# Two residual graph-attention layers on one core: the third of seven products is split into seven small ones too, and tiles and PSUM banks are shared out anew

## The chip, the core and the metric

The kernel runs on one NeuronCore of a Trainium2 chip. The metric is the device time of one execution in microseconds (us), the median of several runs. Five engines work side by side, each through its own queue in order: TensorE (PE) multiplies matrices and writes into PSUM, VectorE (DVE) and ScalarE (ACT) read PSUM and work elementwise, GpSimd (POOL) works elementwise on SBUF, and SyncE (SP) issues the DMA transfers here. They wait for each other by semaphores. [...]

## The reference

There are 128 graphs of 128 nodes with 512 features, one adjacency matrix `adj` for all of them, and two layers in fp32. Cut to what matters:

```
# layer 0
q, k, v = x @ Wq0.T, x @ Wk0.T, x @ Wv0.T
rel = adj.T * (q @ k.T);  rel = rel / norm(rel, axis=2)
x1  = layernorm(x + rel @ v)
# layer 1: 8 heads of 64
q, k, v = x1 @ Wq1 + bq1, x1 @ Wk1 + bk1, x1 @ Wv1 + bv1
w   = softmax(q_h @ k_h.T / 8 + where(adj == 0, -1e9, 0))
out = layernorm(x1 + concat_h(w @ v_h))
```

## The kernel before

**Groups and projections.** The kernel takes four graphs at a time: 32 groups `g` of 512 tokens. Wq0 and Wk0 are multiplied into one matrix at the start, so a group needs five products of a 512 x 512 weight with its 512 x 512 tokens: `m` and `v0` in layer 0, `q`, `k` and `v1` in layer 1. Each is an instance of `Projection`, 160 in all.

**Seven products.** A projection is not done as eight products of halves but as seven, P1 to P7 (Winograd's form of Strassen's scheme), on sums of weights (`wc`, seven tiles made once, `weight_sums`) and on sums of tokens (`tx` and `tx1`, four tiles made for each group by `token_sums`). `product` issues one of them as four matmuls of 256 columns (L327). P1, P6, P7 and P4 go into bank `a` in turn and partly add up there, P5 and P3 into bank `b`. `empty` copies a bank to SBUF on ACT (L335, L338); `add` adds a bank to an SBUF tile on DVE (L342).

**P2 is made from seven products of quarters.** The second product is split once more in the same way: `inner_product` issues one matmul of 128 columns (L360), `inner` does seven of these in four steps of 3, 2, 1 and 1 and adds each to the projection's output on DVE (L374 to L390). They use sums of weight quarters (`wd`, `inner_weight_sums`) and of token quarters (`ux`, L234 to L237, on POOL). All seven share three slots of one bank `pc`. In group 0 `m` and `v0` are plain: their P2 is four ordinary matmuls.

**Order.** Nothing is left to a scheduler: the emission order is a list of steps. A round `r` has 35 steps, seven for each projection. `dense` holds the projections' products at fixed places in those seven (P1 at 0, P5 at 1, P6 at 3, P3 at 5, P7 at 6, P4 at 9, that is at 2 of the next one), with the inner steps at the places of `INNER`. `short` holds everything else at places that hand-set tables give: `ZERO` for layer 0, `STEADY`, `QUICK` and `LAST` for the softmax and output of layer 1 in ordinary rounds, the last but one group, and the last. Round `r` makes `m` and `v0` of group r+1, and `q`, `k`, `v1` of group r; the softmax of a group runs on into the next two rounds. Each engine takes its own instructions in this order.

**Softmax and rows.** For each graph `b` of a group: `attn_scores` (PE into banks `ps`, then DVE), `attn_max` (DVE), `attn_exp` (ACT), `attn_spill` and `attn_stage` (DMA to HBM and back, for a layout), `attn_transpose` (DVE into `wT`), `attn_out` (PE into `po`, then DVE), `attn_back` and `attn_rows` (DMA to HBM and back: rows `o` of softmax times v, and rows `xr` of x1), `attn_sum` (DVE multiplies `o` by the softmax's divisors, POOL adds the bias and `o` to `xr`), `attn_stats`, `attn_norm`, `attn_write`. Layer 0 has `l0_score` (banks `pst`), `l0_norm` (bank `pn`, from squares `sq` made on POOL), `l0_out`, `l0_rstd`, `l0_layernorm`; `x1_spill` and `x1_stage` bring x1 to HBM and back for `x1_transpose`, `x_transpose` does the same for the next x.

**Buffers.** Eight PSUM banks: two of `ps_a` (bank `a`), one of `ps_b` (bank `b`), five of `ps_m` (all else). SBUF tiles are named by tags; a tile with a tag used before waits for the end of all use of the tile before it. `o` and `xr` have two tiles each of their own, and `self.s`, half of which holds P5 and half P6, has a tile with the tag `s`.

Of the kernel before, what the change touches and what calls it, by code (L numbers as in the profile page):

```python
# [18 lines left out]
def kernel(  # L19
# [32 lines left out]
    ps_b = ctx.enter_context(tc.tile_pool(name="ps_b", bufs=1, space=bass.MemoryType.PSUM))  # L52
    ps_m = ctx.enter_context(tc.tile_pool(name="ps_m", bufs=5, space=bass.MemoryType.PSUM))
# [87 lines left out]
    wd = {n: const.tile([P, 3, P], F32, name=f"wd_{n}") for n in wc}  # L141

    def inner_weight(key, i):
        if i >= 5:
            return wd[key][:, i - 5]
        e, d = {1: (0, 0), 2: (0, 1), 3: (1, 0), 4: (1, 1)}[i]
        return wc[key][:, 1, d, e * P:(e + 1) * P]

    def inner_weight_sums(key, eng):
        w = [None] + [inner_weight(key, i) for i in range(1, 8)]  # L150
        eng.tensor_tensor(w[5], w[3], w[4], op=ALU.add)
        eng.tensor_tensor(w[6], w[5], w[1], op=ALU.subtract)
        eng.tensor_tensor(w[7], w[1], w[3], op=ALU.subtract)
        eng.tensor_tensor(w[3], w[2], w[6], op=ALU.subtract)
# [63 lines left out]
    def token_sums(t, xT, dh):  # L218

        if dh == 0:  # L220
            nc.vector.tensor_tensor(t[:, 0], quarter(xT, 0, 1), quarter(xT, 0, 0), op=ALU.subtract)
        else:
            nc.vector.tensor_tensor(t[:, 1], quarter(xT, 1, 1), t[:, 0], op=ALU.subtract)
            nc.gpsimd.tensor_tensor(t[:, 2], quarter(xT, 1, 1), quarter(xT, 0, 1), op=ALU.subtract)
            nc.gpsimd.tensor_tensor(t[:, 3], quarter(xT, 1, 0), t[:, 1], op=ALU.subtract)

    def inner_token(xT, i):
        d, t = {1: (0, 0), 2: (1, 0), 3: (1, 1), 5: (0, 1)}[i]
        return xT[:, 2 + d, t, :]

    def inner_token_sums(u, xT):

        eng = nc.gpsimd
        eng.tensor_tensor(u[:, 0], inner_token(xT, 5), inner_token(xT, 1), op=ALU.subtract)  # L234
        eng.tensor_tensor(u[:, 1], inner_token(xT, 3), u[:, 0], op=ALU.subtract)
        eng.tensor_tensor(u[:, 2], inner_token(xT, 3), inner_token(xT, 5), op=ALU.subtract)
        eng.tensor_tensor(u[:, 3], inner_token(xT, 2), u[:, 1], op=ALU.subtract)  # L237

    def x_inner(g):
        UX[g] = one.tile([P, 4, P], F32, tag="ux", name=f"ux_{g}")  # L240
        inner_token_sums(UX[g], XT[g])

    def x1_inner(g):
        UX1[g] = one.tile([P, 4, P], F32, tag="ux1" if g < NG - 1 else "ux", name=f"ux1_{g}")
        inner_token_sums(UX1[g], X1T[g])

    def x_transpose(g, dh, h):
        if dh == 0 and h == 0:

            XT[g] = one.tile([P, C, G, P], F32, tag="xT" if g else "x1T", name=f"xT_{g}")  # L250
            TX[g] = one.tile([P, 4, 2, HF], F32, tag="tx" if g else "tx1", name=f"tx_{g}")
        transpose_quarter(XT[g], g, h, dh)
        if h:
            token_sums(TX[g], XT[g], dh)
# [11 lines left out]
    def x1_transpose(g, dh, h):  # L266
        if dh == 0 and h == 0:

            X1T[g] = one.tile([P, C, G, P], F32, tag="x1T" if g < NG - 1 else "xT", name=f"x1T_{g}")
            TX1[g] = one.tile([P, 4, 2, HF], F32, tag="tx1" if g < NG - 1 else "tx", name=f"tx1_{g}")  # L270
        transpose_quarter(X1T[g], g, h, dh)
        if h:
            token_sums(TX1[g], X1T[g], dh)

    def graph(g, b):
        return X[g, b // 2][:, b % 2, :]

    class Projection:
# [8 lines left out]
        def begin(self):  # L287
# [5 lines left out]
            if k == "v1":  # L293

                self.s0 = one.tile([P, 2, HF], F32, tag="rel", name=f"s0_{self.name}")
# [3 lines left out]
            self.s = one.tile([P, 2, 2, HF], F32, tag="s", name=f"s_{self.name}")  # L299
# [41 lines left out]
        def add(self, eh, th, bank, s):  # L341
            nc.vector.tensor_tensor(self.out(eh, th), bank, self.s[:, s], op=ALU.add)  # L342

        def quarters(self, j):

            y = self.y.rearrange("p a b -> p (a b)" if self.wide else "p c b n -> p (c b n)")
            y = y.rearrange("p (j n) -> p j n", n=P)
            s0 = y if self.kind != "v1" else self.s0.rearrange("p m (t n) -> p (m t) n", n=P)
            w = C if self.kind != "v1" else 2
            e, t = j  # L350
            if not self.wide:
                e, t = t, e
            i, k = e + t * C, e + t * w
            return (y[:, i], s0[:, k]) if j != (1, 1) else (y[:, 0:i + 1:i], s0[:, 0:k + 1:k])

        def inner_product(self, i, slot, start=False):
            l, r = inner_weight(self.kind, i), self.u[:, {5: 0, 6: 1, 7: 2, 4: 3}[i]] if i >= 4 else inner_token(self.xT, i)
            if self.wide:
                l, r = r, l
            nc.tensor.matmul(self.c[:, slot, :], l, r, start=start, stop=True, skip_group_check=True)  # L360

        def inner(self, n):

            add = nc.vector.tensor_tensor
            self.u = (UX if self.kind in ("m", "v0") else UX1)[self.g]
            if n == 0:
                if self.kind == "v1":
                    self.place()
                self.c = ps_m.tile([P, 3, P], F32, tag="m", name=f"pc_{self.name}")
                self.inner_product(1, 0, True)  # L370
                self.inner_product(5, 1)
                self.inner_product(2, 2)
                y, s0 = self.quarters((1, 1))
                add(y, self.c[:, 0:2], s0, op=ALU.add)  # L374
                y, _ = self.quarters((0, 0))
                add(y, self.c[:, 2], y, op=ALU.add)
            elif n == 1:
                self.inner_product(6, 0)
                self.inner_product(3, 1)
                y, s0 = self.quarters((0, 1))  # L380
                add(y, self.c[:, 0], s0, op=ALU.add)
                add(y, self.c[:, 1], y, op=ALU.add)
            elif n == 2:
                self.inner_product(7, 0)
                y = self.last_quarter()
                add(y, self.c[:, 0], y, op=ALU.add)
            else:
                self.inner_product(4, 0)
                y, s0 = self.quarters((1, 0))
                add(y, self.c[:, 0], s0, op=ALU.add)  # L390

        def last_quarter(self):
            return self.quarters((1, 1))[0][:, 1]

        def step(self, i):
            if i == 1:
                self.begin()
                self.a = ps_a.tile([P, 2, HF], F32, tag="a", name=f"pa_{self.name}")
                self.product(1, self.a, True)
                self.empty(self.s0, self.a, 0)  # L400
            elif i == 5:
                self.b = ps_b.tile([P, 2, HF], F32, tag="b", name=f"pb_{self.name}")
                self.product(5, self.b, True)
                self.empty(self.s[:, 0], self.b, 1)
            elif i >= 10:
                if not self.plain:
                    self.inner(i - 10)
            elif i == 2:
                if self.plain:
                    d = ps_m.tile([P, 2, HF], F32, tag="m", name=f"pd_{self.name}")  # L410
                    self.product(2, d, True)
                    nc.vector.tensor_tensor(self.s0, d, self.s0, op=ALU.add)
            elif i == 6:
                self.product(6, self.a, False)
                self.empty(self.s[:, 1], self.a, 0)
            elif i == 3:
                self.product(3, self.b, False)
                self.add(0, 1, self.b, 1)
            elif i == 7:
                self.product(7, self.a, False)  # L420
                self.add(1, 1, self.a, 0)
# [150 lines left out]
    def attn_rows(g, b):  # L572
        o = two.tile([P, A, H // 2, Q], F32, tag="o", name=f"o_{g}_{b}")
        nc.sync.dma_start(o.rearrange("p f a r -> p (f a r)"), OD.pop((g, b)).rearrange("p f d -> p (f d)"))
        xr = two.tile([P, D], F32, tag="xr", name=f"xr_{g}_{b}")
        nc.sync.dma_start(xr, X1D[g, b // 2][b % 2])
        SOFT[g, b] = o, xr, SOFT[g, b][1]

    def attn_sum(g, b):

        o, xr, rs = SOFT[g, b]
        f = o.rearrange("p f a r -> p (f a) r")
# [4 lines left out]
        nc.gpsimd.tensor_tensor(xr_, xr_, o, op=ALU.add)  # L587
# [92 lines left out]
    def last_store(g, b):  # L680
# [13 lines left out]
        ((10.5, 10.5, 10.5, 11), 13.5, (22.5, 21.5, 20, 19.5), 24, (28.5, 27), (31, 30.5), (35, 32.5), (38, 40.5, 42.5, 44.5)),  # L694
# [3 lines left out]
        (32, (35.5, 35.5, 36, 36, 36), (36, 36), 41.5, (43.5, 49, 49, 52, 56.5, 59.5, 61, 62.5)),  # L698
        (32, (32.5, 40, 40, 42, 42), (40, 42.5), 44.5, (47, 49, 50, 53, 59, 65, 66, 68.5)),
        (49, (50.5, 50.5, 50.5, 52, 52), (52, 54.5), 54.5, (59, 67, 67.5, 69.5, 75, 78, 78, 80)),  # L700
        (49, (53, 53, 54, 56, 57), (59, 59), 61, (65, 67, 68.5, 71.5, 76.5, 82, 82, 83.5)),
    )
    QUICK = (
        (31.5, (32, 33.5, 33.5, 34, 36), (33.5, 36), 40.5, (42, 43.5, 44, 47.5, 48.5, 50.5, 52, 52.5)),
        (35.5, (36, 37, 37, 37, 37), (39.5, 39.5), 41, (45.5, 47.5, 47.5, 50, 52.5, 53.5, 55.5, 62.5)),
        (36, (38, 41, 41, 41, 41), (41, 41), 45.5, (47.5, 52, 57.5, 57.5, 57.5, 59, 61.5, 64)),
        (37.5, (39, 40, 44, 49, 49), (46, 49), 51.5, (53, 54.5, 60, 63, 63, 67.5, 68.5, 68.5)),
# [128 lines left out]
```

## Time and profile before

| | us |
|---|---|
| runs | 2457.88, 2459.82, 2459.85 |
| median | 2459.82 |
| profiled execution, its own time | 2458.22 |
| its span in the trace | 2456.3 |
| granted TensorE clock, mean | 0.998 |

The page of the profiled execution gives each engine's busy time, share of the span and count of instructions. A group's row names a line of the kernel, the engine, the operation, output and inputs with their shapes, how often it ran, its busy time, the mean duration of one in ns, the idle time just before it, and what ended that. A row of waits is: who waited for whom, total us, times, longest. Matmul records overlap, so what one costs is read from the distance of starts. An fp32 matmul shows as two records, each with a weight load (PEld).

### The profile page before, as it was taken

To read this page: it belongs to the slowest core of one execution; us is meant where nothing else is said; L and a number is where in the kernel's file an instruction comes from. 1 tells how busy PE (TensorE), PEld (TensorE's weight loads), DVE (VectorE), ACT (ScalarE), POOL (GpSimd) and SP (SyncE) were. 2 spreads that over 40 slices of the span, in tenths; PEclk is the share of its full clock that TensorE was granted. 3 is DMA by queue.
4 is the path that set the end of the run, shared out by engine and by line. 5 is a ranking of instruction groups with operands and counts; after the bars stand their busy time and mean duration, and the time that the engine had idled before them with its cause. 6 is when DMAs were issued, how large, how long until landed. Compare 5 with 4: busy or idle time off the path is not lost.

```text
span 2456.3 us, 44484 instructions
## 1 busy us (share of the span) xinstructions
PE 2435.0 (99%) x15604; PEld 2123.7 (86%) x15604; DVE 1738.2 (71%) x3505; ACT 1000.4 (41%) x3211; POOL 952.3 (39%) x1478
## 2 busy tenths in 40 slices
PE   8999999999999999999999999999999999999997
PEld 6888888888888888888888888888888888888886
DVE  5566777767777767777677777677776777776777
ACT  1234343433443343434434443434344343434354
POOL 4423433434434334334344343443333433434434
PEclk9999999999999999999999999999999999999999
DMA  7446656666565666556665656655566556566564
GB/s 160 104 129 183 164 161 169 164 183 171 162 165 157 173 187 164 163 162 165 187 165 165 171 153 174 189 163 163 159 164 189 158 166 172 158 176 182 150 172 133
DMA packets 508577, 404.93 MB, mean 165 GB/s; under 512 B 37568, under 2 KB 424768, under 8 KB 508352
## 3 DMA queue, kind: packets, MB, share of 16 engines
q1 hardware_dynamic: 508352, 402.08, 60.2%
q8 instruction: 122, 2.00, 0.4%
q14 instruction: 103, 0.84, 0.1%
HBM read 237.31 MB, written 164.63 MB: 164 GB/s over the span
## 4 chain that ended last, share of the span: by engine, by line
PE 98%; DVE 1%; POOL 0%; issue 0%; DMA 0%; POOLq 0%; ACT 0%; SPq 0%; DVEq 0%
PE pa_v L327 18%; PE pa_q L327 9%; PE pa_k L327 9%; PE pa_m L327 9%; PE pb_v L327 9%; PE ps L499 5%; PE po L557 5%; PE pst L434 5%; PE pb_q L327 5%; PE pb_k L327 4%; PE pb_m L327 4%; PE po L479 4%; PE pc_v L360 4%; PE pc_q L360 2%; PE pc_k L360 2%; PE pc_m L360 2%
## 5 line engine op out<-in xcount | busy, mean ns | idle before, releaser
L585 POOL TENSOR_TENSOR xr<-xr,bv_b 128x512 f32<-128x512 f32 x124 | 158.4, 1278 | 626.0 <-DMA xr<-x1d 204.8
L525 ACT ACTIVATE w<-w,nmax 128x128 f32<-128x128 f32 x992 | 384.2, 392 | 11.7 <-DVE nmax L518 11.7
L587 POOL TENSOR_TENSOR xr<-xr,o 128x512 f32<-128x512 f32 x124 | 157.5, 1270 | 532.7 <-issue 457.5
L327 PE MATMUL pa_v<-wc_v,tx 128*128 128x256 f32 x1536 | 363.7, 380 | 0.0
L327 PEld LDWEIGHTS pa_v<-wc_v,tx 128*128 128x128 f32 x1536 | 282.1, 190 | 33.7
L474 ACT ACTIVATE xr<-xr,sh,rstd 128x512 f32<-128x512 f32 x124 | 100.9, 814 | 377.6 <-POOL sh L469 377.4
L525 ACT ACTIVATION_READ_ACCUMULATOR w<-w,nmax 128x1 f32 x992 | 189.1, 191 | 0.0
L327 PE MATMUL pa_m<-tx,wc_m 128*128 128x256 f32 x768 | 181.7, 379 | 0.8 <-DVE yT L342 0.8
L327 PE MATMUL pa_k<-tx,wc_k 128*128 128x256 f32 x768 | 181.7, 379 | 0.0
L327 PE MATMUL pa_q<-tx,wc_q 128*128 128x256 f32 x768 | 181.6, 379 | 0.0
L327 PEld LDWEIGHTS pa_q<-tx,wc_q 128*128 128x128 f32 x768 | 143.3, 190 | 43.8 <-issue 28.9
L508 DVE SCALAR_TENSOR_TENSOR w<-ps,mask 128x512 f32<-128x512 f32 x248 | 154.2, 684 | 15.6 <-PE ps L499 15.6
L338 ACT ACTIVATE qT<-pa_q,bq_sb 128x256 f32<-128x256 f32 x128 | 53.6, 470 | 271.9 <-PE pa_q L327 271.9
L544 DVE STREAM_TRANSPOSE wT<-wl 128x1024 f32<-128x1024 f32 x124 | 154.0, 1242 | 5.7 <-DMA wl<-wd 4.6
L518 DVE TENSOR_REDUCE nmax<-w 128x4 f32<-128x512 f32 x248 | 157.2, 676 | 0.0
L327 PEld LDWEIGHTS pa_m<-tx,wc_m 128*128 128x128 f32 x768 | 141.1, 190 | 17.8 <-DVE yT L342 1.2
L327 PEld LDWEIGHTS pa_k<-tx,wc_k 128*128 128x128 f32 x768 | 141.0, 190 | 16.6 <-issue 0.2
L560 DVE STREAM_TRANSPOSE oT<-po 128x512 f32<-128x512 f32 x124 | 88.8, 716 | 79.5 <-PE po L557 76.0
L335 ACT COPY yT<-pa_m 128x512 f32<-128x512 f32 x64 | 37.7, 590 | 231.2 <-PE pa_m L327 231.2
L499 PE MATMUL ps<-kT,qT 64*128 64x128 f32 x1984 | 129.5, 279 | 0.0
L499 PEld LDWEIGHTS ps<-kT,qT 64*128 64x128 f32 x1984 | 117.4, 187 | 11.2 <-issue 10.8
L479 PE MATMUL po<-v,rel 128*128 128x512 f32 x256 | 125.4, 592 | 0.0
(229 smaller groups left out, 5432.9 us busy)
## 6 DMA issues: line engine op xcount, KB each, us to landing
wd<-w SPq DMA_DIRECT2D x248, 256.0 KB, 3.1
wl<-wd SPq DMA_DIRECT2D x496, 128.0 KB, 3.1
xl_x<-in_x_dram SPq DMA_DIRECT2D x256, 128.0 KB, 6.7
x<-in_x_dram SPq DMA_DIRECT2D x64, 512.0 KB, 4.9
x1d<-x SPq DMA_DIRECT2D x64, 512.0 KB, 2.8
xl_h<-x1d SPq DMA_DIRECT2D x256, 128.0 KB, 3.5
od<-oT SPq DMA_DIRECT2D x496, 64.0 KB, 1.8
o<-od SPq DMA_DIRECT2D x124, 256.0 KB, 3.2
```

What stands on the lines that cost most here:

```text
L327: nc.tensor.matmul(bank[:, m, :], l[:, k, m * P:(m + 1) * P], r[:, k, :], start=start and m == 0 and k == 0, stop=(m == 1 and k == 1), ski ...
L360: nc.tensor.matmul(self.c[:, slot, :], l, r, start=start, stop=True, skip_group_check=True)
L434: nc.tensor.matmul(p, XT[g][:, dc, b, :], YT[g][:, dc, b, :], start=(dc == 0), stop=(dc == C - 1))
L479: nc.tensor.matmul(p, REL[g][0][:, b, :], V0[g][:, b, :], start=True, stop=True)
L499: nc.tensor.matmul(p[s][:, :, a, :], QT[g][r, a, b, :], KT[g][r, a, b, :], start=True, stop=True)
L508: nc.vector.scalar_tensor_tensor(w[:, s].rearrange("p q a r -> p (q a r)"), p[s].rearrange("p q a r -> p (q a r)"), HD ** -0.5, mask, op0= ...
L518: nc.vector.tensor_reduce(nmax[:, s * (H // 2):(s + 1) * (H // 2)], w[:, s].rearrange("p q a r -> p a q r"), axis=AX.XY, op=ALU.max, negat ...
L525: nc.scalar.activation(w[:, s, :, a, :], w[:, s, :, a, :], AF.Exp, bias=nmax[:, i:i + 1], accum_out=sums[:, i:i + 1])
L544: nc.vector.transpose(wT, SOFT[g, b][0].rearrange("p a i r -> p i a r"))
L557: nc.tensor.matmul(p[s * HD:(s + 1) * HD, a, :], V1[g][:, b, h * HD:(h + 1) * HD], wT[:, s * (H // 2) + a].rearrange("p q t -> p (q t)"), ...
L585: nc.gpsimd.tensor_tensor(xr, xr, bv_b, op=ALU.add)
L587: nc.gpsimd.tensor_tensor(xr_, xr_, o, op=ALU.add)
```

## The change

P3 is split as P2 is. `inner_weight`, `inner_weight_sums`, `inner_token`, `inner_token_sums` and `inner` get a number `o` (2 or 3) for the outer product. `wd` and `ux` double, and there are two banks `pc2` and `pc3` in place of `pc`. The plain projections make P3 with four ordinary matmuls in a bank of its own.

Since P3 no longer adds up in bank `b`, the sums are formed elsewhere: P5 is copied twice (`s01`, `s11`), P6 is added to `s01` on DVE and no longer copied by ACT, P7 is added to `s11`. For `v1` (but for the last group) these two lie in a shared tile (`shared`), for the others in the projection's own output, so that the tag `s` goes. The shared tile has the tag `yT` and also holds the rows `xr` of graphs 0 and 1; `room` places the other rows `o` and `xr` in tiles with the tags `tx` and `x`, and at the end in the weights of `m` and `v0`. The tags `o` and `xr` go.

`attn_rows` is cut in two: `attn_res`, which loads `xr`, comes at step `RES` = 59 for graphs 0 and 1. The first token sum is made on POOL from the third group of x on, and for x1; the inner weight sums of `v0` and `m` are made on DVE, those of the others later. `ps_b` goes and `ps_m` has six banks. Places in `ZERO`, `STEADY`, `QUICK` and `LAST` are changed, a few by several steps; the order of P1, P5, P6, P7 and P4 is not.

```
-    ps_b = ctx.enter_context(tc.tile_pool(name="ps_b", bufs=1, space=bass.MemoryType.PSUM))
-    ps_m = ctx.enter_context(tc.tile_pool(name="ps_m", bufs=5, space=bass.MemoryType.PSUM))
+    ps_m = ctx.enter_context(tc.tile_pool(name="ps_m", bufs=6, space=bass.MemoryType.PSUM))
...
     def inner_weight_sums(key, eng):
+        for o in (2, 3):
+            w = [None] + [inner_weight(key, o, i) for i in range(1, 8)]
+            eng.tensor_tensor(w[5], w[3], w[4], op=ALU.add)
...
+    def token_sums(t, xT, dh, eng=nc.gpsimd):
         if dh == 0:
-            nc.vector.tensor_tensor(t[:, 0], quarter(xT, 0, 1), quarter(xT, 0, 0), op=ALU.subtract)
+            eng.tensor_tensor(t[:, 0], quarter(xT, 0, 1), quarter(xT, 0, 0), op=ALU.subtract)
...
         transpose_quarter(XT[g], g, h, dh)
+        if dh == 1 and g:
+            inner_token_sums(UX[g], XT[g], 2 + h)
         if h:
-            token_sums(TX[g], XT[g], dh)
+            token_sums(TX[g], XT[g], dh, nc.gpsimd if g > 1 else nc.vector)
...
+    def shared(r):
+        if r not in SX:
+            t = one.tile([P, 2, 2, D], F32, tag="yT", name=f"sx_{r}")
+            SX[r] = t[:, 0], t[:, 1].rearrange("p s (m e) -> p s m e", m=2)
+        return SX[r]
...
+    def room(g, b, of):
+        if g >= NG - 2 or (g == NG - 3 and b >= 2):
+            i = 2 * b + of if g == NG - 2 else 6 + 2 * b + of
+            t = wc["m" if i < 7 else "v0"].rearrange("p i k e -> p (i k e)")
+            return t[:, i % 7 * D:(i % 7 + 1) * D]
+        if b < 2 and of:
+            return shared(g + 1)[0][:, b]
...
+        def middle(self):
+            if self.late:
+                s = shared(self.g)[1]
+                return s[:, 0], s[:, 1]
+            return self.out(0, 1), self.out(1, 1)
...
+        def inner(self, o, n):
+            def add(slot, j, kept=True):
+                y, s = self.quarters(o, j)
+                nc.vector.tensor_tensor(y, self.c[o][:, slot], s if kept else y, op=ALU.add)
...
+            if n == 0:
+                self.c[o] = ps_m.tile([P, 3, P], F32, tag="m", name=f"pc{o}_{self.name}")
+                self.inner_product(o, 1, 0, True)
+                self.inner_product(o, 5, 1)
+                self.inner_product(o, 2, 2)
+                add(slice(0, 2), (1, 1))
+                add(2, (0, 0), False)
+            elif n == 1:
+                self.inner_product(o, 6, 0)
+                self.inner_product(o, 3, 1)
+                add(0, (0, 1))
+                add(1, (0, 1), False)
+            elif n == 2:
+                self.inner_product(o, 7, 0)
+                y = self.quarters(o, (1, 1))[0][:, 1]
+                nc.vector.tensor_tensor(y, self.c[o][:, 0], y, op=ALU.add)
+            else:
+                self.inner_product(o, 4, 0)
+                add(0, (1, 0))
...
             elif i == 5:
-                self.b = ps_b.tile([P, 2, HF], F32, tag="b", name=f"pb_{self.name}")
+                self.b = ps_m.tile([P, 2, HF], F32, tag="m", name=f"pb_{self.name}")
                 self.product(5, self.b, True)
-                self.empty(self.s[:, 0], self.b, 1)
+                self.s01, self.s11 = self.middle()
+                self.empty(self.s01, self.b, 0)
+                self.empty(self.s11, self.b, 1)
...
             elif i == 6:
                 self.product(6, self.a, False)
-                self.empty(self.s[:, 1], self.a, 0)
+                add(self.s01, self.a, self.s01, op=ALU.add)
             elif i == 3:
-                self.product(3, self.b, False)
-                self.add(0, 1, self.b, 1)
+                if self.plain:
...
             elif i == 7:
                 self.product(7, self.a, False)
-                self.add(1, 1, self.a, 0)
...
+                add(self.out(1, 1), self.a, self.s11, op=ALU.add)
...
-        ((10.5, 10.5, 10.5, 11), 13.5, (22.5, 21.5, 20, 19.5), 24, (28.5, 27), (31, 30.5), (35, 32.5), (38, 40.5, 42.5, 44.5)),
+        ((10.5, 10.5, 10.5, 11.5), 13.5, (19.5, 21.5, 22.5, 17.5), 23.5, (26, 28), (29, 29.5), (30, 31.5), (37.5, 38.5, 41, 44.5)),
...
     STEADY = (
-        (32, (35.5, 35.5, 36, 36, 36), (36, 36), 41.5, (43.5, 49, 49, 52, 56.5, 59.5, 61, 62.5)),
-        (32, (32.5, 40, 40, 42, 42), (40, 42.5), 44.5, (47, 49, 50, 53, 59, 65, 66, 68.5)),
-        (49, (50.5, 50.5, 50.5, 52, 52), (52, 54.5), 54.5, (59, 67, 67.5, 69.5, 75, 78, 78, 80)),
-        (49, (53, 53, 54, 56, 57), (59, 59), 61, (65, 67, 68.5, 71.5, 76.5, 82, 82, 83.5)),
+        (32, (32.5, 34.5, 35, 35, 35), (35, 37), 41.5, (44, 49, 51.5, 56, 60, 64.5, 68, 68)),
+        (32, (35.5, 38.5, 38.5, 41.5, 41.5), (41.5, 41.5), 42, (47.5, 49, 51, 52, 61.5, 65, 69, 69)),
+        (49, (49.5, 49.5, 52.5, 52.5, 52.5), (55, 55), 57.5, (58, 67, 67, 70, 73, 75, 77, 77)),
+        (49, (50.5, 55, 55, 55, 55), (56.5, 58), 60.5, (64.5, 67, 69, 74.5, 76, 82, 83, 85.5)),
     )
...
     INNER = (
-        (2.71, 6.22, 8.23, 9.24),
-        (4.21, 8.72, 9.23, 9.74),
-        (2.21, 4.22, 6.73, 8.24),
+        (2.71, 3.72, 8.23, 9.24, 3.26, 7.27, 8.28, 9.29),
+        (5.71, 8.72, 9.23, 9.74, 5.26, 7.27, 8.28, 8.79),
+        (2.71, 3.22, 6.73, 8.74, 2.76, 5.27, 7.28, 8.79),
     )
+
+    RES = 59
```

The first four entries of an `INNER` row are P2's steps, the last four P3's; the rows are for `m`, `v0`, `q` and `k`, for `v1`, and for the last round.

## The prediction

> **What bounds the kernel now.** I read the page's busy times first, then who waits for whom, then TensorE in order of time, then busy times by stretch.
>
> ```profile
> PE 2435.0 (99%) x15604; PEld 2123.7 (86%) x15604; DVE 1738.2 (71%) x3505; ACT 1000.4 (41%) x3211; POOL 952.3 (39%) x1478
> PE 98%; DVE 1%; POOL 0%; issue 0%; DMA 0%; POOLq 0%; ACT 0%; SPq 0%; DVEq 0%
> ```
>
> The second line is the chain that ended last: nearly all of the span is TensorE (PE) working, not waiting. The waits confirm it. The first two lines below are the longest of PE's, the others the longest of VectorE's (DVE): PE waits about 13 us in all, and DVE mostly waits for PE.
>
> ```profile
> PE pM L193 <- DMA wk_s<-in_L_gnn_Wk_dram: 4.4, 1, 4.4
> PE po L557 <- DVE wT L544: 1.5, 1, 1.5
> ...
> DVE v L386 <- PE pc_v L360: 111.7, 61, 2.4
> DVE rel L435 <- PE pst L434: 92.0, 127, 3.5
> ```
>
> So PE's own work sets the time. Its price is read from the starts (first column) in the order of time:
>
> ```profile
> 1004.53 0.38 PE L360 MATMUL pc_q<-ux,wc_q 128*128 128x128 f32 x2
> 1004.76 0.39 PE L360 MATMUL pc_k<-x1T,wc_k 128*128 128x128 f32 x2
> 1004.98 0.39 PE L360 MATMUL pc_k<-ux,wd_k 128*128 128x128 f32 x2
> 1005.20 0.39 PE L360 MATMUL pc_k<-x1T,wc_k 128*128 128x128 f32 x2
> 1005.43 1.89 PE L327 MATMUL pa_k<-tx,wc_k 128*128 128x256 f32 x8
> 1007.15 1.89 PE L327 MATMUL pb_k<-x1T,wc_k 128*128 128x256 f32 x8
> 1008.88 1.89 PE L327 MATMUL pa_k<-tx,wc_k 128*128 128x256 f32 x8
> 1010.61 0.39 PE L360 MATMUL pc_k<-ux,wd_k 128*128 128x128 f32 x2
> ```
>
> Every matmul is two records. Three outer products of four matmuls each take 1010.61 - 1005.43 = 5.18 us: 1.727 us a product, 0.432 a matmul of 256 columns. Four matmuls of 128 columns take 1005.43 - 1004.53 = 0.90: 0.225 each.
>
> The stretches give a steady round (first line; 75.2 us is also the distance of equal steps in the chain) and the end. Columns: window, its length, then busy us of PE, PEld, DVE, ACT, POOL.
>
> ```profile
> 1000.00:1075.20 75.20, 75.20 (x488) 65.90 (x487) 53.79 (x109) 31.03 (x101) 28.96 (x46) 1.00 0.63 174
> 2400.00:2420.00 20.00, 20.00 (x140) 17.12 (x136) 12.53 (x26) 9.04 (x25) 7.62 (x15) 1.00 0.69 201
> 2420.00:2442.00 22.00, 18.60 (x159) 16.07 (x158) 21.01 (x40) 15.12 (x68) 9.69 (x14) 1.00 0.32 94
> ```
>
> In a round DVE has 21 us to spare. From 2420 on it is DVE that is full: the end belongs to DVE.
>
> [...] the trace starts a 128-column pass every 112 ns, [...] though each load record lasts 190. [...] GpSimd (POOL) is about twice as slow on an elementwise add; the trace has 1.27 to 1.72 us against 0.69.
>
> **The change, part by part.** The sum is against the profiled execution, 2458.2 us (span 2456.3 and 1.9 around it); the median of the three runs, 2459.8, lies 1.6 above it.
>
> *PE.* Of 160 projections 158 are not plain. Each loses P3's four matmuls, 4 x 0.432 = 1.727, and gets seven small ones, 7 x 0.225 = 1.575: 0.152 saved; with the shorter spacing of 0.22 seen after 1010.61 it is 0.187. I take 0.163, **25.8 us** in all, 0.81 a round of five; bounds 24 to 29.
>
> *DVE, added.* P3's six adds per projection:
>
> ```profile
> L374 DVE TENSOR_TENSOR kT<-pc_k,kT 128x256 f32<-128x256 f32 x32 | 13.6, 425 | 15.7 <-PE pc_k L360 15.7
> L376 DVE TENSOR_TENSOR kT<-pc_k,kT 128x128 f32<-128x128 f32 x32 | 9.3, 291 | 1.1
> L342 DVE TENSOR_TENSOR kT<-pb_k,s_k 128x512 f32<-128x512 f32 x32 | 21.9, 684 | 1.3 <-PE pb_k L327 1.3
> ```
>
> 0.425 + 5 x 0.29 = 1.87 us, 9.4 a round. P3's 512-column add (third row) goes, and P6's takes its place (it was a ScalarE (ACT) copy): zero. The first token sum moves to POOL, -0.7 twice a round. DVE goes from 53.8 to 61.7 us of a 74.4-us round, 83%. All of it lies beside PE's work as long as no PE step finds its add missing; that is the question below.
>
> *ACT.* P5 is emptied twice (0.58 each), P6 no more: zero. *POOL.* Four more inner sums of 0.455 and a token sum of 1.7, twice a round: 29 + 7 = 36 us of 74. POOL's nearest deadline is the norm's matmuls, which need the squares. Its queue ahead of them: the two row pairs of the second half (each waits for its DMA and for DVE), a token sum, eight inner sums, two token sums. With the trace's durations the last square ends about 0.8 us ahead of PE. I charge nothing; if the row transfers land 1 us late it costs up to 1 us a round.
>
> *DMA and SP.* The same transfers. The residual rows of b < 2 go out at step 59, behind the last softmax spill, whose landing SP waits for since they lie in the same tile; the weight stage queues behind them. With the softmax's 0.58 us an exponential on ACT, 0.45 us an issue and 3.1 us a landing, the stage of b = 2 lands some 3 us before DVE's transpose of it, that of b = 3 some 8: hidden, nothing. Without that cover DVE, and PE behind it, would wait up to 3 us a round. Steps 29 to 31.5 (spill and stage of x1) move earlier by a slot or more and still wait for the buffer's transposes. The first weight tile's rows wait for v0's P4 to free tx; one round's slack, nothing.
>
> *PSUM.* pb joins the pool, so it serves three tiles a projection in place of one and lends a bank for 13 us to each of two. Those that reuse them (pst, ps) come after their adds by 2 us or more: nothing; unknown either way, -1 to +6 us overall.
>
> *Shared tiles.* In a round v1's two middle parts and the rows x1 of b < 2 lie in the tile that yT takes next. So ACT's copy of m's P1 now waits for v1's last P3 add and for the output writes; the copies of P5 and v1's P4 queue behind it. The add ends about 5.5 us into the round, the copy at 6.1, and P6, which needs it, starts at 7.6: nothing; a DVE late by more than 1.4 us there would stop PE by the rest.
>
> *New waits of PE.* I lay DVE's queue against PE's starts, adds back to back about 0.08 shorter than their duration, as in DVE's timeline. (a) P7 now waits for P6's DVE add. Where nothing stands between (m, k), PE has the two small steps, 0.67 + 0.45 = 1.12 us; the add ends 0.69 + about 0.2 of pipeline after P6, and the next load starts a pass early: slack 0.05 to 0.1. Behind the waiting P7 is all of PE. In v0 the scores, in q the l0 outputs, in v1 attention stand between. (b) v1's tail, in the next round: P3's seventh product, then two small products of P2 (0.45), then P3's fourth into the same slot. DVE must first finish the maxima (1.27 us) and then add 0.29: PE waits 0.2 to 0.3. (c) The other inner pairs have an outer product between: nothing. So 0.25 x 31 = **7.8 us lost**; bounds 0 (DVE ahead) to 25 (all of the gain).
>
> *Start and end.* Weight sums of v0 and m go to DVE (16 x 0.29 = 4.6), beside PE's wait for the first yT, and leave POOL: 0 to +1.5, I take 1. At the end DVE is full and v1's extra adds stand in it: 1.87, I take **+2**; those of q and k fit into the 7.5 us free at 2400 to 2420.
>
> Sum: 2458.2 - 25.8 + 7.8 + 1 + 2 = 2443.2; beside the median, **2444.8**, and I say 2444.
>
> **Rivals.** A measurement of this kernel tells 0.2%, 4.9 us, from no change: faster is below 2454.9, slower above 2464.7.
>
> *A, no new waits.* Adds are always there: 2459.8 - 25.8 + 2 = 2436. For: DVE's idle time is mostly waiting for PE. Against: (b). Counted with the forecast's case, together 0.63.
>
> *B, part of the gain lost.* Waits of 0.5 to 0.65 a round leave 2449 to 2455: 0.13. At 0.65 to 0.95, nothing is seen: 2455 to 2464, 0.08.
>
> *C, slower: P7 behind P6's add.* At m and k one DVE instruction in front at the wrong moment (a row product or transpose, 0.69, or the softmax transpose, 1.24) stops PE for 0.6 and 1.2: 1.8 a round. Net +1.0 x 31 with start and end: 2459.8 + 31 + 3 = 2494; it decides from 0.81 us of waiting a round. For: slack of 0.1 us, an in-order queue at 83%, row products that wait for DMA right ahead of m's P6 add. Against: those rows land some 5 us before. 0.15.
>
> *D, the small products aren't cheaper.* If a pass took its load record's 190 ns, seven would cost 2.66: 2459.8 + 158 x 0.93 = 2607. The starts exclude it: 0.01.
>
> **How the numbers follow.** Faster 0.63 + 0.13 = 0.76; same 0.08; slower 0.15 + 0.01 = 0.16. The range starts at 2433 (A, with the higher saving) and ends at 2464: what is left out is most of C and D and a little below.
>
> **What would show it.** PE's spacing stays 0.432 and 0.225; the round shrinks to 74.4 plus the waits; PE waits name L405 or L454 adds of DVE. Right: one wait of 0.2 to 0.3 a round at v1's P3 and little at P7. Wrong: P7 waiting at m or k, PE waiting for POOL's squares, or a weight stage or row that lands late; a round of 75.2 or more refutes the forecast.

## The result, and the profile after

The changed kernel takes **2447.61 us** (median of 4 runs, 2445.90 to 2451.50); the kernel before took 2458.94 beside it (4 runs, 2457.88 to 2459.85). The ratio is **0.9956**, 95% interval 0.9939 to 0.9974: faster by 0.44%. The forecast was 2444, with 2433 to 2464 as its range. The profiled execution is the slowest of the four, 2451.5 us with a span of 2449.7.

First the busy times and the chain of waits, from the page:

```profile
PE 2423.1 (99%) x16552; PEld 2133.5 (87%) x16552; DVE 1976.5 (81%) x4409; ACT 1012.1 (41%) x3211; POOL 1138.9 (46%) x1796
PE 96%; DVE 2%; DMA 1%; issue 0%; POOL 0%; SPq 0%; POOLq 0%; ACT 0%; DVEq 0%
```

PE has 948 matmul records more and 12 us of busy time less; DVE has risen from 71% to 81% of the span. PE still sets the time. Who waits for whom (engine, line, releaser; us in total, times, longest; the view lists no wait under 0.15 us):

```profile
DVE v L405 <- PE pc_v L399: 73.9, 156, 1.6
DVE rel L478 <- PE pst L477: 49.1, 96, 3.2
...
PE pM L193 <- DMA wk_s<-in_L_gnn_Wk_dram: 4.3, 1, 4.3
PE pa_m L358 <- DVE yT L454: 3.0, 1, 3.0
...
PE pc_v L399 <- DVE v L425: 1.9, 1, 1.9
PE po L701 <- DVE wT L686: 1.4, 2, 1.0
```

Two lines of PE matter. Each counts one wait, so neither recurs from round to round: the 3.0 us, new, stand in the start; the 1.9, 0.6 before, in the last v1 at the end. Then k on PE, in order of time (start, duration):

```profile
1006.92 0.39 PE L399 MATMUL pc_k<-x1T,wc_k 128*128 128x128 f32 x2
1007.15 1.89 PE L358 MATMUL pa_k<-tx,wc_k 128*128 128x256 f32 x8
1008.88 0.38 PE L399 MATMUL pc_k<-x1T,wc_k 128*128 128x128 f32 x2
...
1009.77 0.39 PE L399 MATMUL pc_k<-x1T,wc_k 128*128 128x128 f32 x2
1009.99 1.90 PE L358 MATMUL pa_k<-tx,wc_k 128*128 128x256 f32 x8
1011.73 1.89 PE L358 MATMUL pa_v<-wc_v,x1T 128*128 128x256 f32 x8
```

An outer product still takes 1.73 us (1008.88 - 1007.15), and five small products take 1.11 (1009.99 - 1008.88), 0.222 each. The second `pa_k` is P7 and starts with no wait: P6's add is there in time. By stretches (window, length, then busy us of PE, PEld, DVE, ACT, POOL; then the granted clock, which is the share of its full clock that TensorE was given, the DMA share and GB/s):

```profile
1000.00:1074.66 74.66, 74.48 (x516) 65.82 (x515) 60.91 (x137) 31.47 (x100) 34.85 (x55) 1.00 0.61 167
2400.00:2420.00 20.00, 19.82 (x159) 17.22 (x158) 17.45 (x38) 8.75 (x31) 8.34 (x14) 1.00 0.65 187
2410.00:2432.00 22.00, 18.91 (x167) 16.39 (x166) 21.01 (x43) 12.76 (x58) 7.35 (x13) 1.00 0.33 98
```

A round lasts 74.66 us, 0.54 less than before. In it DVE works 60.9 us (forecast 61.7) and POOL 34.9 (forecast 36). At the end DVE is full, as before.

**Where the time went.** I cut both traces at the first matmul of q's P1 in the first and in the last round. All times are spans in us; the third column is the changed kernel profiled again (experiment 5, total 2445.04).

| stretch | before | after | after again |
|---|---|---|---|
| start, to q of round 0 | 83.0 | 90.6 | 83.9 |
| 31 rounds, to q of the last | 2296.5 | 2279.8 | 2279.8 |
| the rest | 76.8 | 79.3 | 79.3 |
| span | 2456.3 | 2449.7 | 2443.1 |

The rounds give 16.7 us in both, the end costs 2.5 in both. The start costs 7.6 us in one execution and 0.9 in the other.

The start of the slow one, on DVE (start, duration): the eight inner weight sums of v0, which the change brought here, at their fifth to eighth, and behind them P6's add of m.

```profile
41.48 0.28 DVE L151 TENSOR_TENSOR wd_v<-wc_v 128x128 f32<-128x128 f32 x1
41.79 1.24 DVE L152 TENSOR_TENSOR wd_v<-wd_v,wc_v 128x128 f32<-128x128 f32 x1
42.96 1.34 DVE L153 TENSOR_TENSOR wd_v<-wc_v 128x128 f32<-128x128 f32 x1
44.33 1.23 DVE L154 TENSOR_TENSOR wc_v<-wc_v,wd_v 128x128 f32<-128x128 f32 x1
45.49 0.68 DVE L454 TENSOR_TENSOR yT<-pa_m,yT 128x512 f32<-128x512 f32 x1
```

And on PE (the bracket gives PE's idle time just before, and who ended it):

```profile
46.23 3.05 PE L358 MATMUL pa_m<-tx,wc_m 128*128 128x256 f32 x8 [3.04 <-DVE yT L454]
50.13 3.78 PE L358 MATMUL pa_m<-tx,wc_m 128*128 128x256 f32 x8 [0.85 <-DVE yT L464]
```

The eight sums took 6.8 us in place of 2.3: six of them take 0.58 to 1.34 us where 0.28 is normal. P7 of m therefore waited 3.04 us, and it and P4 then took 3.05 and 3.78 us in place of 1.89: from 47.01 to 53.84 us the granted clock was 0.50. It was so once more from 60.66 to 64.07.

### The profile page after: what moved, and what is told of

It is laid out like the page before. It is cut to its first block, busy times and chain, and to the rows that moved or that the text cites. A ratio compares the mean times of both kernels' runs of the same rounds, so it can differ in the third digit from the quotient of the medians.

```text
span 2449.7 us, 48441 instructions
## 1 busy us (share of the span) xinstructions
PE 2423.1 (99%) x16552; PEld 2133.5 (87%) x16552; DVE 1976.5 (81%) x4409; ACT 1012.1 (41%) x3211; POOL 1138.9 (46%) x1796
## 4 chain that ended last, share of the span: by engine, by line
PE 96%; DVE 2%; DMA 1%; issue 0%; POOL 0%; SPq 0%; POOLq 0%; ACT 0%; DVEq 0%
PE pa_v L358 18%; PE pa_q L358 9%; PE pa_m L358 9%; PE pa_k L358 9%; PE pc_v L399 8%; PE ps L542 5%; PE po L600 5%; PE pst L477 5%; PE pb_v L358 5%; PE po L522 4%; PE pc_k L399 4%; PE pc_q L399 4%; PE pc_m L399 4%; PE pb_q L358 2%; PE pb_k L358 2%; PE pb_m L358 2%
## 5 line engine op out<-in xcount | busy, mean ns | idle before, releaser
L502 POOL TENSOR_SCALAR ve<-st 128x1 f32<-128x1 f32 (+1 forms) x160 | 45.9, 287 | 745.4 <-DVE st L498 735.3
L517 ACT ACTIVATE xr<-xr,sh,rstd 128x512 f32<-128x512 f32 x58 | 47.2, 814 | 411.3 <-POOL sh L512 411.3
L358 PE MATMUL pa_m<-tx,wc_m 128*128 128x256 f32 x768 | 186.8, 387 | 4.1 <-DVE yT L454 3.0
L405 DVE TENSOR_TENSOR v<-pc_v,v 128x256 f32<-128x256 f32 (+1 forms) x444 | 135.2, 310 | 58.3 <-PE pc_v L399 46.4
L631 POOL TENSOR_TENSOR xr<-xr,bv_b 128x512 f32<-128x512 f32 x58 | 73.7, 1271 | 146.1 <-DMA xr<-x1d 79.1
L399 PE MATMUL pc_v<-wd_v,ux 128*128 128x128 f32 x756 | 135.8, 275 | 0.2 <-DVE v L405 0.2
L405 DVE TENSOR_TENSOR qT<-pc_q,qT 128x128 f32<-128x128 f32 (+1 forms) x320 | 96.5, 309 | 44.4 <-PE pc_q L399 36.7
L522 PE MATMUL po<-v,rel 128*128 128x512 f32 x256 | 130.7, 594 | 0.0
```

The lines of the kernel that those rows point to most:

```text
L358: nc.tensor.matmul(bank[:, m, :], l[:, k, m * P:(m + 1) * P], r[:, k, :], start=start and m == 0 and k == 0, stop=(m == 1 and k == 1), ski ...
L399: nc.tensor.matmul(self.c[o][:, slot, :], l, r, start=start, stop=True, skip_group_check=True)
L405: nc.vector.tensor_tensor(y, self.c[o][:, slot], s if kept else y, op=ALU.add)
L522: nc.tensor.matmul(p, REL[g][0][:, b, :], V0[g][:, b, :], start=True, stop=True)
L631: nc.gpsimd.tensor_tensor(xr, xr, bv_b, op=ALU.add)
```

## The experiments

Each was timed beside the kernel before, on the same chip (which took 2458.5 to 2459.5 us there). "Round" and "start" are read from q's first matmuls, as above.

**1. v0's sums behind m's.** Is it the place of the sums that costs the start?

```
-    for k, name, eng in ((9, "v0", nc.vector), (17, "m", nc.vector), ...
+    for k, name, eng in ((17.5, "v0", nc.vector), (17, "m", nc.vector), ...
```

> The eight inner weight sums of v0 stay on VectorE (DVE) but stand behind those of m, at step 17.5 of the start in place of 9. Theory (the start was mis-sized because the sums ran on DVE beside GpSimd's (POOL) layer-1 sums and PE's P7 of m waited behind them): each of the eight takes 0.28 to 0.3 us, m's P7 has no wait (3.0 us in the changed kernel), the granted clock stays at 1.00 there, round 0's first q product starts 6 to 7 us earlier (83.5 to 85 us in place of 90.6), and the whole is 5 to 7 us faster than the changed kernel: 2440 to 2443. Rival (the start is late because the first transfer landed 1.1 us later and the clock fell for its own reasons): the wait moves or stays, the clock falls again, less than 1.5 us of the total changes: 2446 to 2449.

Measured: 2444.30 us (5 runs, 2444.01 to 2447.03), ratio 0.9945 (0.9932 to 0.9957). Start 84.9. PE in the start:

```profile
43.41 1.89 PE L358 MATMUL pa_m<-tx,wc_m 128*128 128x256 f32 x8
46.16 1.99 PE L358 MATMUL pa_m<-tx,wc_m 128*128 128x256 f32 x8 [0.85 <-DVE yT L464]
...
54.62 3.31 PE L358 MATMUL pa_m<-xT,wc_m 128*128 128x256 f32 x8 [1.11 <-DVE xT L212]
```

P7 (43.41) no longer waits and P4 runs at full clock; each of the eight sums takes 0.28 or 0.29. So the wait belonged to the sums. The gain in the median is 3.3 us, less than the 5 to 7 expected, and the two intervals of the ratio overlap: not every execution of the changed kernel has a start as long as the profiled one (83.9 in the table). The clock fell here too: it averages 0.66 from 55 to 60 us, behind a wait of only 1.11 us that every kernel has, and the product there took 3.31 us. Not all of the lost clock comes from the sums. Single starts scatter besides: this same start took 82.5, 86.0, 82.7 and 86.2 us in the profiles of experiments 6, 7, 11 and 12.

**2. v1's tail one outer product earlier.** Wait (b) of the prediction shows on PE as two gaps of 0.1 us, one before P3's fourth product and one behind it. Are they DVE's?

```
-        (5.71, 8.72, 9.23, 9.74, 5.26, 7.27, 8.28, 8.79),
+        (5.71, 8.72, 9.23, 9.74, 5.26, 6.27, 7.28, 8.29),
```

> Three small steps of v1's P3 move one outer product earlier (6.27, 7.28 and 8.29 in place of 7.27, 8.28 and 8.79), so that an outer product stands between its seventh and its fourth product. Theory (wait (b) is PE behind DVE's add before the fourth product): the two gaps of 0.1 us at v1's tail go and nothing takes their place, a steady round takes 74.45 us in place of 74.66, the whole is 5 to 7 us faster: 2441 to 2443. Rival 1 (the gaps are PE's own, at the change from one bank or shape to another): the round stays at 74.66, the whole at 2447 to 2449. Rival 2 (the third and sixth products, now straight behind P7, wait for DVE instead): the round is 74.7 to 75, the whole 2448 to 2458.

Measured: 2459.84 us (13 runs), ratio 1.0005 (0.9997 to 1.0013); a round takes 74.97. The two gaps are gone, but PE now stops where P3's third and sixth product stand straight behind P7:

```profile
877.04 1.89 PE L358 MATMUL pa_v<-wc_v,tx 128*128 128x256 f32 x8
879.18 0.49 PE L399 MATMUL pc_v<-wd_v,ux 128*128 128x128 f32 x2 [0.25 <-DVE v L405]
```

The gap before 879.18 is 0.41 us and the next 0.1. Here DVE was busy with two softmax maxima (1.26 us from 877.21) and came to P3's first add at 878.39. Rival 2 held: the gaps are DVE's, and a new wait larger than the old one took their place. The 31 rounds take 2290.8 us, 11.0 more than in the changed kernel but still 5.7 less than before; with the longer start (88.4) and end (79.7) nothing of the gain was left. Both ranges of a total were missed, Rival 2's by 2 us: the last of the 31 intervals alone grew by 1.4 us.

**3 and 4. P3 plain in one kind.** What does P3 bring in v1, where the waits are, and in q, where none are? The diff is that for v1; for q it names "q". In both kernels the plain P3 multiplies by a weight block that the inner sums have overwritten; the instructions and their sizes are as stated.

```
...
             elif i == 3:
-                if self.plain:
+                if self.plain or self.kind == "v1":
...
+                    add(self.out(0, 1), d, self.s01, op=ALU.add)
```

> P3 of v1 alone is made again from four matmuls of 256 columns into a bank of its own, with one add of 512 columns; all other kinds keep the seven products. Theory (v1's P3 saves 0.163 us and gives 0.2 back as wait (b), and 2 us at the end, where DVE is full): the round gets 0.163 longer and loses the 0.2 of waits, so 31 x -0.04 = -1 us, and the end is 1 to 2 us shorter: 2 to 3 us faster than the changed kernel, 2444 to 2446. Rival (v1's P3 brings its full share): 32 x 0.163 = 5.2 us slower, 2452 to 2453.

> P3 of q alone is made again from four matmuls of 256 columns, as before the change, into a bank of its own. Theory (each projection with P3 made from seven products saves 0.163 us of PE, and q's have no waits): 32 x 0.163 = 5.2 us slower than the changed kernel, 2452 to 2454, a round of 74.82 in place of 74.66. Rival (q's saving is hidden by waits elsewhere, or the small products cost more than their spacing shows): less than 2 us either way.

Measured: v1 plain 2445.62 us (5 runs, 2443.69 to 2448.12), ratio 0.9946 (0.9933 to 0.9960), round 74.62, the rest 77.3. q plain 2452.84 us (8 runs, 2449.32 to 2454.72), ratio 0.9974 (0.9964 to 0.9984), round 74.82, the rest 79.1. Both theories held to 0.01 us a round: one projection's P3 saves 0.16 us a round, v1's gives 0.2 back to its waits and costs 2 us more at the end. In v1 the change brings nothing.

**5. The changed kernel again.**

> The changed kernel once more, unaltered, on the chip that runs the next ones, as their measure. 2446 to 2449; its P7 of m in the start waits 2 to 3 us again if the wait belongs to the order of VectorE's queue and not to one run.

Measured: 2448.32 us (5 runs, 2445.04 to 2450.69), ratio 0.9959 (0.9945 to 0.9973). P7 of m waited 1.81 us in its profile, a little less than the 2 to 3 expected, and no product behind it was slowed. With the first four this makes nine runs, and the mean granted clock orders them: at 0.999 they took 2445.0, 2445.9 and 2446.4 us, at 0.998 2446.6, at 0.997 2448.3 to 2451.5, at 0.996 2450.7.

**6. v1's P2 one place later** (with v0's sums behind m's).

```
-        (5.71, 8.72, 9.23, 9.74, 5.26, 7.27, 8.28, 8.79),
+        (8.72, 9.23, 9.74, 10.25, 5.26, 7.27, 8.28, 8.79),
```

> The sums of v0 stand behind m's (as in the first experiment), and v1's four steps of P2 move one place later, 8.72, 9.23, 9.74 and 10.25: so P2's first three small products stand between P3's seventh and fourth, where two stood, and P2's last one between m's P6 and P7. Theory (wait (b) is DVE's add, late by 0.2 us there, and (a) is P6's add, late by 0.07): three small products for two add 0.22 us of cover at (b), one more adds 0.22 at (a): both waits go, a round takes 74.40 us in place of 74.66, the whole is 8 us faster than the kernel of the first experiment: about 2436 to 2438. Rival (the queue of DVE only shifts, so that P6's add comes later by the adds moved in front of it): a new wait at m's P7 of 0.2 to 0.5 us, a round of 74.6 to 75.0.

Measured: 2445.71 us (5 runs, 2444.13 to 2446.63), ratio 0.9946 (0.9934 to 0.9958), round 74.70. Both waits that were aimed at went: (b), with 0.89 us of small products in front of the fourth, and (a). A new one came, at P2's seventh product, 0.2 us before it and 0.1 behind it, and that, not m's P7 as the rival had it, ate the gain. The timeline tells its size: the last of the two products it needs starts at 876.32, their adds run at 876.75 and 877.07, and the seventh starts at 877.42. From start to start that is 1.10 us, where PE had 0.89 to do.

**7. v0's sums behind m's, and v1's P3 plain**: the edits of the first and the third together, with v1's weights kept.

```
+        for o in (2, 3) if key != "v1" else (2,):
```

> The sums of v0 stand behind m's, and v1's P3 is four matmuls of 256 columns again, its weights kept as they are. Theory (v1's P3 gains nothing in a round and costs 2 us at the end; the start costs its 5 us on its own): round 74.62, end about 77.3, the whole 2 to 3 us below the kernel of the first experiment, 2441 to 2443. Rival (the gain of v1 plain seen before was the scatter of one chip): equal to the first experiment within 1 us, or slower.

Measured: 2443.26 us (5 runs, 2441.22 to 2444.63), ratio 0.9935 (0.9923 to 0.9948), on the chip where the changed kernel took 2448.32. Round 74.62, the rest 77.3. The theory held.

**8. POOL idle beside the sums.** The sums of v0 stay at their place; POOL's work on q's weights moves.

```
-                for name, key in (("v", "v1"), ("q", "q")):
-                    layer1_weights(name, key)
+                layer1_weights("v", "v1")
...
+    at(-1, 26, layer1_weights, "q", "q")
```

> The inner sums of v0 stay where the change puts them on DVE; POOL's seven operations on the layer-1 weights of q move from the start of m to step 26, so that POOL is idle while DVE makes the sums. Theory (DVE's adds took 1.2 to 1.3 us in place of 0.28 because POOL worked on the same memory, and only so were late for m's P7): each takes 0.28 to 0.3, the eight end about 41.2 us, m's P7 waits less than 0.5 us, the clock stays up there; 3 to 6 us faster than the changed kernel. Rival (the place in the queue alone makes the wait; the adds are slow for another reason, such as their weights' addresses): they take 1.2 us again and P7 waits 2 to 3 us.

Measured: 2450.03 us (4 runs, 2449.14 to 2451.12), ratio 0.9964 (0.9951 to 0.9978). The same sums on DVE, at the same place of the queue:

```profile
38.44 0.29 DVE L152 TENSOR_TENSOR wd_v<-wd_v,wc_v 128x128 f32<-128x128 f32 x1
38.65 0.28 DVE L153 TENSOR_TENSOR wd_v<-wc_v 128x128 f32<-128x128 f32 x1
38.97 0.29 DVE L154 TENSOR_TENSOR wc_v<-wc_v,wd_v 128x128 f32<-128x128 f32 x1
```

All eight take 0.28 or 0.29 us, and m's P7 has no wait. So it was POOL working at the same time that stretched them, not their place or their addresses. The total was missed: POOL's moved work ends at 73.1 us, the layer norm's scale behind it at 74.9, ACT's normalisation at 75.1 in front of v0's copies, and PE waits there:

```profile
PE pa_v L358 <- ACT v L366: 4.1, 1, 4.1
```

**9. One more DVE instruction in front of P6's add**, in m and k: the dose for rival C.

```
                 self.product(6, self.a, False)
+                if self.kind in ("m", "k") and self.g > 0:
+                    add(mask, mask, mask, op=ALU.max)
```

> One more DVE instruction of 512 columns (the maximum of the mask with itself, which changes nothing) stands right in front of P6's add in m and k of every group but the first: the case that the slower rival of the prediction was about. Theory (P7 of m and k has nothing but 1.12 us between it and P6, and a slack of about zero): PE stops for 0.6 to 0.7 us at each of the two, 1.3 us a round, round 75.9 to 76.1, the whole about 40 us slower than the changed kernel: 2482 to 2492. Rival (DVE begins the extra instruction early, in idle time before P6 ends, so that it is hidden): less than 5 us slower; at m this is likelier than at k, since DVE stood idle 0.35 us before m's P6 add.

Measured: 2480.08 us (4 runs, 2477.45 to 2481.28), ratio 1.0086 (1.0072 to 1.0099); a round takes 75.73, 1.07 more. The sum is a little below what was expected, its parts are far from equal: 0.9 us at k and 0.15 at m. At m the instruction takes 0.68 us and DVE's idle time in front of P6's add hides most of it. At k it takes 1.71 to 1.76 us in 27 of 31 rounds. DVE, POOL and PE there, three answers of the timeline:

```profile
865.09 1.75 DVE L455 TENSOR_TENSOR mask<-mask 128x512 f32<-128x512 f32 x1
866.77 0.68 DVE L456 TENSOR_TENSOR kT<-pa_k,kT 128x512 f32<-128x512 f32 x1
```

```profile
865.03 1.27 POOL L633 TENSOR_TENSOR sx<-sx,bv_b 128x512 f32<-128x512 f32 x1
```

```profile
867.50 0.70 PE L358 MATMUL pa_k<-tx,wc_k 128*128 128x256 f32 x2 [0.65 <-DVE kT L456]
```

POOL's addition of the residual's bias began 0.06 us earlier, and the DVE instruction took 1.07 us longer than at m. So a kernel slower than before is one instruction away, as rival C had it, but not by its sum: C charged 0.6 us for an instruction of 0.69, and at m, where it took 0.68, it cost 0.15. What cost 0.9 at k is the instruction stretched beside POOL.

**10. The sums back on POOL**, both at step 17.

> Undo of the part of the change at the start: the inner sums of v0 and m stay on POOL and both at step 17, as the kernel before had them, but now sixteen in place of eight. Theory (POOL's 16 x 0.455 = 7.3 us stand in front of the squares that PE's norm needs): m's P7 has no wait, but PE waits for POOL's squares some 4 to 5 us more; the start is 2 to 4 us longer than with the sums on DVE behind m's; about as slow as the changed kernel, 2445 to 2452. Rival (POOL has finished before the squares come): start as short as before, 2441 to 2444.

Measured: 2447.13 us (4 runs, 2446.18 to 2450.15), ratio 0.9955 (0.9940 to 0.9971), start 84.0. The rival was right on the start: POOL ends the sums at 50.6 us, and PE waits 0.9 for the squares, as in every kernel. The total came out within the theory's band for another reason: in this execution the rest takes 81.7 us, with a granted clock of 0.80 to 0.86 from 2410 on. So moving the sums to DVE bought nothing that shows in the start, and cost the wait.

**11. The maxima behind the tail** (with v0's sums behind m's). The prediction laid (b) to the softmax maxima in front of the add.

```
-        (32, (35.5, 38.5, 38.5, 41.5, 41.5), (41.5, 41.5), 42, ...
+        (32, (37.1, 38.5, 38.5, 41.5, 41.5), (41.5, 41.5), 42, ...
```

> The sums of v0 stand behind m's, and the two maxima of the softmax of b = 1 (1.27 us of DVE) move from step 35.5 to 37.1, from in front of the add of P3's seventh product in v1's tail to behind the add of its fourth. Theory (wait (b) is that add, queued behind these maxima): the two gaps of 0.1 us at v1's tail go, the round is 74.45 in place of 74.66, the whole 6 us less than the kernel of the first experiment: 2438 to 2440. Rival 1 (the add is late by the way from PE to DVE and back, whatever stands in front of it): gaps stay, 74.66. Rival 2 (the maxima delay another add of P2 or m's P6): the wait moves, 74.6 to 75.0.

Measured: 2445.67 us (5 runs, 2443.58 to 2446.84), ratio 0.9946 (0.9933 to 0.9958), round 74.66: both gaps are there unchanged. PE, and DVE beside it:

```profile
873.74 0.61 PE L399 MATMUL pc_v<-wd_v,ux 128*128 128x128 f32 x4
874.18 0.39 PE L399 MATMUL pc_v<-wc_v,x1T 128*128 128x128 f32 x2
874.51 0.49 PE L399 MATMUL pc_v<-wc_v,ux 128*128 128x128 f32 x2
```

```profile
874.16 0.29 DVE L425 TENSOR_TENSOR v<-pc_v,v 128x128 f32<-128x128 f32 x1 [1.33 <-PE pc_v L399]
```

DVE now stood idle 1.33 us, and still the add of the seventh product (PE, 873.74) began only at 874.16 and the fourth at 874.51. Rival 1 held: the wait is the way from PE to DVE and back. It is 0.42 us to the add, 0.29 of add and 0.06 back, 0.77 from start to start, where the three small products from the seventh on last 0.67.

**12. The tail spread by that rule** (with v0's sums behind m's).

```
-        (5.71, 8.72, 9.23, 9.74, 5.26, 7.27, 8.28, 8.79),
+        (8.72, 9.23, 10.1, 10.73, 5.26, 7.27, 8.28, 8.79),
```

> The sums of v0 stand behind m's, and v1's steps of P2 move to 8.72, 9.23, 10.1 and 10.73. Theory (PE - DVE - PE is a round trip: 0.42 us from the start of a small product to its add, 0.29 of add, 0.06 back, so 0.77 us from start to start, and 1.10 where two adds follow; a wait of 0.1 and 0.1 more for the first matmul after it is what (b) is): at v1's P3 seven to four stand 0.22 + 0.67 = 0.89 us, no wait; P2's seventh product stands behind m's P6, far from the two adds it needs; its fourth after five small products, 1.34 us; m's P6 and P7 are 1.57 us apart. All extra gaps go: a round of 74.39, 8 us less than the kernel of the first experiment, 2436 to 2438. Rival (DVE's queue, not the round trip, is what is late around m's P6): one of the moved products waits 0.2 us or more, a round of 74.6 or longer.

Measured: **2437.72 us** (4 runs, 2436.70 to 2440.38), ratio **0.9910** (0.9894 to 0.9927), round 74.39. The chain in order of time (start, length, what) shows v1's tail and m's P7 of the changed kernel:

```profile
807.21 1.09 PE pc_v L399 x8
808.30 1.73 PE pa_v L358 x8
...
813.99 1.79 PE pa_m L358 x8
```

and the tail in this one:

```profile
799.65 1.11 PE pc_v L399 x10
800.76 1.73 PE pa_v L358 x8
...
806.90 1.73 PE pa_m L358 x8
```

Eight records, four small products, took 1.09 us in place of 0.89; now ten take 1.11, 0.222 a product, and P7 of m takes the bare 1.73. No wait for DVE recurs in the rounds any more; one of 31 has one of 0.2 us. This version is faster than both kernels.

## Why the prediction was right, and where it was off

The direction and the range held, and the median is 3.6 us above the forecast of 2444. By its own steps:

- **PE's saving, 0.163 us a projection: right.** Experiment 4 undoes it for one kind and a round grows by 0.16.
- **Wait (b), 0.2 to 0.3 us a round: size right, cause wrong.** The step that failed is "DVE must first finish the maxima (1.27 us)". They end in time; experiment 11 takes them away and nothing changes. It is the round trip of 0.77 us, and 0.1 us that the first matmul behind the wait costs, of which the step said nothing. That the size came out right is luck. For sizing the cause made no difference, for mending it did: moving the maxima gains nothing, one more small product in between removes it (experiments 6 and 12).
- **Wait (a), P7 behind P6's add: right.** 0.07 us at m, none at k; with (b) 0.27 a round against 0.25. A round shrank by 0.54 us, the forecast's 0.81 less 0.25 being 0.56.
- **Start, +1 us (0 to +1.5): mis-sized.** The term took 0.29 us for each sum and "beside PE's wait for the first yT" as cover. Beside POOL's weight sums the eight of v0 took 6.8 us in place of 2.3 (experiment 8 shows that POOL is the cause), and they stood in front of P6's add, of which the step said nothing: P7 waited 1.8 to 3.0 us. Where the clock held (after again), it put the first product of round 1's m 2.15 us later (55.11 against 52.96), of which 1.2 were won back before q: 0.9 in all. That this is the forecast's figure is luck: the step knew neither the wait nor what was won back, and a single start is not known to 1 us (experiment 1). Where the clock fell, 7.6: by estimate from the two traces 1.1 for a first product of v0 that began later (22.22 against 21.11 us), 3.0 of wait and 4.7 of slow products, less what was won back. The forecast knew no loss of clock; the nine runs show up to 6 us between them with it.
- **End, +2 us: right**, 2.5; it is v1's (experiments 3 and 7: 2 us shorter with v1's P3 plain).
- **PSUM, DMA, SP, POOL, the shared tile: nothing, and nothing that recurs was seen.** One round of 31 is 0.35 us longer than the others, in both profiles of the changed kernel: P6's add of m begins 0.36 us later there (1037.31 us) and P7 waits. The list of waits names a POOL instruction for it, once, 0.2 us; the cause is not known. ACT's copy of m's P1 does begin 0.35 us after v1's last P3 add (883.46 and 883.11 us in one round), and it ends 1.6 us before P6 (885.64); the forecast had 1.5.

Of the rivals, A (no new waits, 2436) is what experiment 12 made true, within 2 us. B's waits of 0.5 us and more a round were not seen; by the prediction's own terms (2459.8 - 25.8 + 1 + 2) its 0.5 to 0.65 would have given 2452 to 2457, not 2449 to 2455. C did not come about: no DVE instruction held up P6's add at k, and experiment 9, which put one there, got a slower kernel, though not by C's sum. D is refuted by the spacing of 0.222.

What stretched the sums shows in other places too. A sum of 128 columns with both inputs in SBUF went from 0.28 to up to 1.34 us beside POOL's operations of 1.27 to 1.40 (changed kernel), a maximum of 512 columns from 0.68 to 1.75 (experiment 9). The rounds of the changed kernel show it too: the row products (`o` times `rs`, two SBUF inputs) take 0.68 us, but up to 1.41 beside POOL, while none of the 1580 inner adds of L405, with one input in PSUM, takes more than 0.43 (0.29 for 128 columns). I had not asked of each added DVE instruction whether both its inputs lie in SBUF.

PE's clock fell after some waits. In the profile of the changed kernel it is 0.50 for 6.83 us behind the wait of 3.0, and for 3.41 us behind one of 1.1. The waits of 2.3 and 2.5 in experiments 2 and 3 were followed by slow products as well (2.64 to 3.78 us in place of 1.89); those of 1.8 to 2.1 us were not, but neither were those of 2.8 and 3.4 in front of v0's first product in experiments 1 and 7. And in 8 of the 14 profiles a product behind a wait of 1.1 us was slow (2.74 to 3.53 us, 1.99 in the others), so the length of one wait is not all of it. What decides between executions stays open.

## What to carry to other kernels

When two engines work hand in hand on one bank, count the round trip from start to start against what stands between, and put that much other work there: here 0.77 us with one add, 1.10 with two. Before an elementwise operation is moved to another engine, ask which operands lie in SBUF and what the neighbour does at that time: the duration from a quiet stretch (0.28 us here) isn't its price (up to 1.34). A wait can cost more than its length: here one of 3.0 us was followed by two products of 3.05 and 3.78 us in place of 1.89.

## What the runs showed of the hardware that was not expected

- A DVE add of 128 columns with both inputs in SBUF: 0.28 us alone (experiment 8), up to 1.34 beside POOL (changed kernel). A maximum of 512 columns: 0.68 and 1.75 (experiment 9); a product of 512 columns: 0.68 and up to 1.41 (changed kernel). An add of 128 columns with one input in PSUM: 0.29 in both cases (changed kernel).
- From the start of a small product on PE to the start of the next one that needs DVE's add of its bank: 0.77 us with one add (experiment 11), 1.10 with two (experiment 6). The first matmul after a wait in the rounds takes PE 0.07 to 0.10 us more (changed kernel: P7 of m 1.96 in place of 1.89, v1's fourth small product 0.49 in place of 0.39).
- In the first 85 us of the changed kernel's profile PE's clock was 0.50 for 6.83 us behind a wait of 3.0 us and for 3.41 behind one of 1.1. Products were slow behind waits of 2.3 and 2.5 us too (experiments 2 and 3), and in 8 of 14 profiles behind the one of 1.1, but not behind ones of 2.8 and 3.4 (experiments 1 and 7).
